# An expert-choice block and a routed block on one core: where the last pair's modulated products run, and when its shared experts run

## The chip, the core and the metric

The kernel runs on one core of one Trainium2 chip. The metric is device time in microseconds, the median of several executions; lower is better. The core has a matmul engine (PE; its weight loads are listed as PEld), a vector engine (DVE), an activation engine (ACT), a general engine (POOL) and a sync engine (SP), which issues most of the DMAs. Each engine works through its own queue in order, and engines wait for one another by semaphores.

## The reference

Eight sequences of 512 tokens with 256 features, fp32, pass through two residual layers.

```python
x = x + ffn0(adapter(x, language))      # 8 experts choose 128 tokens of each sequence
x = x + ffn1(conditioning(x))           # 64 experts, top 8 per token, 128 slots each
                                        # over all 4096 tokens, plus a shared expert
```

The conditioning is the part that matters here. For every sequence:

```python
ctx    = ema(x, tau_ctx)
gated  = x * sigmoid([x, ctx] @ Wg.T + bg)
mod    = 0.5 + sigmoid(gelu(x @ Wn1.T + bn1) @ Wn2.T + bn2)       # 512 x 8
traces = [ema(gated * mod[:, k:k+1], tau[k]) for k in range(8)]
temporal = sum(softmax(blend, 0)[k] * traces[k] for k in range(8))
soma   = gelu(x @ Wsoma.T + bsoma)
out    = layernorm((soma * sigmoid(temporal @ Wtemp.T + btemp)) @ Wout.T)
```

`ema` is the linear recurrence `h = alpha * h + b` along the tokens. Features lie on partitions, tokens along a row, so one recurrence over 128 features is one scan of 128x512. A sequence has 8 rates times 2 halves of the features, so 16 products `gated * mod * blend` and 16 scans. The shared expert of layer 1 is `(silu(x @ Wg) * (x @ Wu)) @ Wd` with 192 hidden features. The routed experts add their weighted results to the rows of their tokens.

## The kernel before

The sequences go in four groups of two. For every group PE first does eight experts of layer 0 (a "unit" is one expert of one group: L694 and L761, then two scatters by POOL, L779, which add the result to `x_rows` in DRAM). When a group's eight units have been scattered, `conditioning(b)` is run for its two sequences, interleaved with the next group's units: SP loads the rows (`xr`, L900), PE transposes them (L274), DVE scans the context `ct` (L959), PE and ACT make the gate (L977, L988), DVE makes `gx` (L996). The modulation `md` goes to DRAM and comes back spread over all partitions as `mdb` (L937 and L947, one load for each two rates). Then come the 16 modulated products `u` (L1037) and scans (L1048). For the first three pairs DVE adds the scans up (L1050); for the last pair, where no units follow, PE adds them in PSUM (L1065, `by_pe`). After this follow the gate of `temporal` (L1085, L1091, L1099), the output (L1120), the statistics and norm (L1133 to L1158), the router scores (L1181) and the shares of the top 8 (`taken`, L1199 to L1227).

`route(g)` collects each expert's tokens in 16 rounds on DVE (L1272, L1273) and a merge of two halves (L1291 to L1297); the second half's list comes by a DMA `rsecond` (L1304). The lists of all experts are turned by PE (L1348, `tkn`) to `ix_c` (L1351), which the first gather waits for.

`shared(b)` loads a sequence's transposed features (`rc1b`, L1372), runs three matmul groups (L1385), silu on ACT (L1391, L1393), a multiplication on DVE (L1397), two matmul groups (L1415), two copies to `rob` (L1420) and a store of the result into the DRAM tensor `odd` (L1429). `odd` and `out` are the two targets of the routed adds: expert e adds into `odd` if e is odd, else into `out`; the store of all eight shared results comes before the first add into `odd`.

`routed(e)` gathers 128 rows by POOL (L1486), transposes, multiplies, and adds by POOL (L1535). Weights come in pairs of experts, 1152 KB each: the first six pairs in a ring `wfar`, which a small POOL copy (L1448) holds back until the last `mdb` is in, and later ones in a ring `wnear` of `NEAR` buffers. `total(b)` reads `odd` and `out` at the end, adds them on DVE and writes `out`.

The order of the work on every engine is not written by hand. A list planner, `Order`, takes steps with an engine, a cost in microseconds, what they read and write, rings of buffers and a rank, and emits them as a simulated schedule starts them; `order.behind(s, x)` lets step `s` start only after `x` in that plan. On the chip only the resulting order of each queue and the semaphores remain. `LATE` names the sequences whose shared result is not stored into `odd` but kept in a buffer `xob` and added in `total`. It is empty here; the code for it is in the file, and for such a sequence zeros are stored to `odd` instead.

Of the kernel before, what the change touches and what calls it, by code (L numbers as in the profile page):

```python
# [8 lines left out]
F32 = mybir.dt.float32  # L9
I32 = mybir.dt.int32  # L10
U32 = mybir.dt.uint32
AF = mybir.ActivationFunctionType
ALU = mybir.AluOpType
# [4 lines left out]
P = 128  # L18
B, S, H = 8, 512, 256
T = B * S  # L20
NL, A = 10, 64
E0, K0, F0 = 8, 128, 1024
# [3 lines left out]
NH = H // P  # L26
PAIR = 2 * 2 * (H // P) * F1 + 3 * H
FAR = 6
NEAR = 8
SPREAD = 3  # L30
WARM = 6
LATE = ()
EPS = 1e-5
NEG = -3.0e38

# [117 lines left out]
def kernel(ctx: ExitStack, tc: tile.TileContext, d: dict, out: bass.AP):  # L153
    nc = tc.nc
# [4 lines left out]
    pools = {"ps": ctx.enter_context(tc.tile_pool(name="ps", bufs=2, space=PSUM))}  # L159
# [55 lines left out]

        "fw1": 2, "fw2": 2, "fb2": 2, "xg": 2 * 2, "exT": 2, "hf": 5, "y": 4,

        "xr": 1, "xb": 2, "hn": 1, "md": 1, "mdb": 5, "ct": 1, "th": 2, "gt": 2, "gx": 2, "so": 2, "tmp": 2, "u": 2, "tr": 2,
        "sg": 1, "c1": 1, "c1T": 1,

        "rlr": 2, "rtk": 1, "rm8": 2, "rev": 1, "rhalf": 1, "rsecond": 1, "rws": 1, "rc1b": 2, "rsl": 1, "rob": 1,

        "wfar": FAR, "wnear": NEAR, "xe": 8, "xhe": 4, "xeT": 3, "xsl": 2, "xheT": 2, "xye": 3, "xob": len(LATE),
    }
# [6 lines left out]
    order = Order(RINGS, ("mm", "hid", "res"))  # L231
    V = {}

    def tile_of(key, ring, shape, dtype=F32):
        place = WHERE.get(ring, "pc")
        if place not in pools:

            was, new = {"pc": (pa_cm, pc_cm), "pm": (pf_cm, pm_cm), "pw": (pc_cm, pw_cm)}[place]
            was.__exit__(None, None, None)
            pools[place] = new.__enter__()  # L240
        V[key] = pools[place].tile(shape, dtype, tag=ring, name=ring, bufs=RINGS[ring])
        return V[key]

    def bank(key, ring="mm"):
        return tile_of(key, ring, [P, 512])

    def pe(cost, fn, **k):
        return order.add("PE", cost, fn, **k)

    def act(cost, fn, **k):  # L250
        return order.add("ACT", cost, fn, **k)

    def dve(cost, fn, **k):
        return order.add("DVE", cost, fn, **k)

    def pool(cost, fn, **k):
        return order.add("POOL", cost, fn, **k)

    def load(size, fn, **k):
        return order.add("SP", 0.1, fn, size=size, **k)  # L260

    KB = 1024
# [38 lines left out]
    NG = len(GROUPS)  # L301
# [6 lines left out]
    def touch(t):  # L308

        nc.gpsimd.memset(t[(slice(0, 1),) * len(t.shape)], 0.0)  # L310
# [304 lines left out]


    units = [(g, e) for g in range(NG) for e in range(E0)]
    weights = []

    def expert(n):  # L620
        u = units[n]
        g, e = u
        bs = GROUPS[g]
        FILL, SOON = 1000 + n, 40
        w1, w2, b2, exT = (k + (u,) for k in (("fw1",), ("fw2",), ("fb2",), ("exT",)))

        def place_1():
            return tile_of(w1, "fw1", [P, NH, F0])

        def place_2():  # L630
            return tile_of(w2, "fw2", [P, NF, H])
# [12 lines left out]
        if n < 2:  # L644
            def hold():
                touch(place_1())
                touch(place_2())

            pool(0.2, hold, new=[(w1, "fw1"), (w2, "fw2")], rank=-1, after=first_rows[:4])
            load(512 * KB, load_1, w=[w1], rank=20 + n)  # L650
            load(512 * KB, load_2, w=[w2], rank=20 + n)
        else:
            weights.append(load(1024 * KB, load_1, new=[(w1, "fw1")], rank=20 + n))
            load(1024 * KB, load_2, new=[(w2, "fw2")], rank=20 + n)
        load(128 * KB, load_3, new=[(b2, "fb2")], rank=20 + n)

        which = 0 if bs[0] in groups[0] else 1
# [92 lines left out]
        for j, b in enumerate(bs):  # L750
            res, y = ("res", u, j), ("y", u, j)
            for part in range(2):
# [13 lines left out]
                need = [w2, b2, *dict.fromkeys(blocks[f][0] for f in fs)]  # L766
# [22 lines left out]
    W = {}  # L789
# [94 lines left out]
    def decay(k):  # L884
        return W["alpha"][:, k : k + 1].to_broadcast([P, S])
# [4 lines left out]
    def conditioning(b):  # L890
        rank = 100 + 5 * b
        g, j = where[b]
        pair = len(GROUPS[g]) == GB
        K = {k: (k, b) for k in (
            "xr", "xb", "hn", "md", "ct", "gx", "so", "tmp", "sg", "mv", "sd", "nm", "c1", "c1T",
        )}
# [8 lines left out]

        s = load(512 * KB, fetch, r=[("x1", b)], new=[(K["xr"], "xr")], rank=rank, after=last_adapter)

        for x in weights[E0 * (g + 1) :][:1]:
            order.behind(x, s)
        turned(K["xr"], K["xb"], "xb", rank, rank)  # L910


# [32 lines left out]
        for k in range(0, D1, 2):  # L945
# [6 lines left out]
            s = load(512 * KB, spread, r=[("md_rows", b)], new=[(("mdb", b, k), "mdb")], rank=rank)  # L952
# [15 lines left out]
        for ec in range(NH):  # L968
            pg, th = ("pg", b, ec), ("th", b, ec)
# [36 lines left out]
        for ec in range(NH):  # L1006
# [15 lines left out]
            new = [(ps, "mm")] + ([(K["so"], "so")] if ec == 0 else [])  # L1022
# [4 lines left out]
        by_pe = b in GROUPS[-1]  # L1027
        for k in range(D1):
            for hc in range(NH):
                mdb, tr, acc = ("mdb", b, k - k % 2), ("tr", b, k, hc), ("acc", b, hc)  # L1030
                tmp = (*K["tmp"], hc)

                def decayed(k=k, hc=hc, mdb=mdb, tr=tr, tmp=tmp):
                    if k == 0 and hc == 0:
                        V["tmp", b] = tile_of(K["tmp"], "tmp", [P, NH, S])
                    u = pools["pc"].tile([P, S], F32, tag="u", name="u", bufs=1)
                    nc.vector.scalar_tensor_tensor(  # L1037
                        u, V[K["gx"]][:, hc, :], W["blend"][:, hc, k : k + 1], V[mdb][:, k % 2, :],
                        ALU.mult, ALU.mult,
                    )  # L1040
                    whole = V[K["tmp"]][:, hc, :]
                    if by_pe:
                        t = tile_of(tr, "tr", [P, S])
                    elif k == 0:
                        t = whole
                    else:
                        t = pools["pc"].tile([P, S], F32, tag="t1", name="t1", bufs=1)
                    nc.vector.tensor_tensor_scan(t, decay(1 + k), u, 0.0, ALU.mult, ALU.add)  # L1048
                    if k and not by_pe:
                        nc.vector.tensor_tensor(whole, whole, t, ALU.add)  # L1050

                need = [K["gx"], mdb, "blend", "alpha"]
                cost = 2.05 if by_pe or k == 0 else 2.75
                if k == 0 and hc == 0:
                    dve(cost, decayed, r=need, new=[(K["tmp"], "tmp")] + ([(tr, "tr")] if by_pe else []),
                        w=[] if by_pe else [tmp], rank=rank)
                elif by_pe:
                    dve(cost, decayed, r=need, new=[(tr, "tr")], rank=rank)
                else:
                    dve(cost, decayed, r=[*need, K["tmp"]], w=[tmp], rank=rank)  # L1060
                if by_pe:
                    def gather_up(k=k, hc=hc, tr=tr, acc=acc):
                        if k == 0:
                            bank(acc, "res")
                        nc.tensor.matmul(V[acc], ident, V[tr], start=k == 0, stop=k == D1 - 1)  # L1065

                    if k == 0:
                        pe(1.0, gather_up, r=[tr], new=[(acc, "res")], rank=rank)
                    else:
                        pe(1.0, gather_up, r=[tr], w=[acc], rank=rank)  # L1070
# [7 lines left out]
        for ec in range(NH):  # L1078
            pgt, gt = ("pgt", b, ec), ("gt", b, ec)
# [15 lines left out]
            def mixed(ec=ec, gt=gt):  # L1095
# [8 lines left out]
               new=[(pgt, "mm"), (gt, "gt")], rank=rank)  # L1104
# [7 lines left out]
        for h, po in enumerate(halves):  # L1112
# [12 lines left out]
            new = [(po, "mm")] + ([(K["c1"], "c1")] if h == 0 else [])  # L1125
# [239 lines left out]
    def shared(b):  # L1365
        rank, soon, soon_dve = 2000 + b, 250 + b, 380 if b in LATE else 45
        c1T, ob = ("c1b", b), ("ob", b)
        ring = "xob" if b in LATE else "rob"

# [35 lines left out]
        for h in range(NC // 2):  # L1405
# [16 lines left out]
            new = [(po, "hid")] + ([(ob, ring)] if h == 0 else [])  # L1422
            lead = [pe(2.0, down, r=[("sh", 0), ("sh", 1), "wsd"], new=new, rank=rank, after=(lead if h else last_tokens if b in LATE else ()))]
            act(0.65, keep, r=[po], w=[ob], rank=soon)

        def store():

            src = zeros.unsqueeze(1).to_broadcast([P, NC, H]) if b in LATE else V[ob]
            nc.sync.dma_start(out=odd[b * S : (b + 1) * S, :].rearrange("(c p) h -> p c h", p=P), in_=src)  # L1429

        load(512 * KB, store, r=() if b in LATE else [ob], w=[("sum", 1, b)], rank=80 if b in LATE else rank)


    def pair(p):

        q = p - FAR
        ring = "wfar" if q < 0 or q % (FAR + NEAR) >= NEAR else "wnear"

# [16 lines left out]
        else:  # L1455
            load(PAIR * P * 3, fetch, new=[(("pair", p), ring)], rank=400 + 2 * p, after=last_tokens if p < FAR + NEAR else ())

# [9 lines left out]
    def give_up(e):  # L1467

        n, rest = divmod(e - 1, SPREAD)
        if e > 0 and rest == 0 and n + FAR + NEAR < E1 // 2:  # L1470
            def touched():
                nc.scalar.copy(spare, V["pair", n][:1, :1])
# [127 lines left out]
    for n in range(len(units)):  # L1600
        expert(n)
# [94 lines left out]
```

## Time and profile before

| | |
|---|---|
| median of 3 runs | 1174.95 us |
| lowest, highest | 1170.82, 1175.83 us |
| the profiled execution | 1181.5 us |
| its span | 1179.7 us |
| mean granted PE clock in it | 0.946 |
| PE busy | 1027.9 us, 87% |
| DVE busy | 682.0 us, 58% |
| ACT busy | 484.7 us, 41% |
| POOL busy | 382.1 us, 32% |
| DMA traffic | 221.75 MB, mean 188 GB/s |

The time is that of one execution as the device counts it. The span runs from the first to the last recorded instruction of the profiled execution; 1.8 us lie around it. Busy times count computing instructions, not waits and not the issue of plain DMAs; POOL's include its indirect DMAs, whose descriptors it prepares. In the lines of a timeline the columns are start, duration, engine, line and operation, output and inputs, the number of instructions, and in brackets the idle time of the engine before it with what ended it.

### The profile page before, as it was taken

Reading aid. Unit: us, or ns where it says so; the run is one execution under the profiler, and the core shown is the slowest. Engines: PE = TensorE matmul, PEld = TensorE weight load, DVE = VectorE, ACT = ScalarE, POOL = GpSimd, SP = SyncE. Lnnn points to the kernel's source line nnn. Section 1 sums busy time; section 2 is a strip of 40 time slices with the busy share of each in tenths; the row PEclk is TensorE's granted clock in tenths of the full one; section 3 lists DMA queues with packets and bytes.
Section 4 is the critical chain, followed back from the end, with each engine's and each line's share of the span. In section 5 each row is a group of like instructions: output and inputs, shape, how many; then the busy total and the mean of one; then the engine's idle time right before and its main releaser. Section 6 shows DMA issues by size and latency. Waiting matters only on the chain.

```text
span 1179.7 us, 13091 instructions
## 1 busy us (share of the span) xinstructions
PE 1027.9 (87%) x4325; PEld 758.5 (64%) x4325; DVE 682.0 (58%) x1447; ACT 484.7 (41%) x1029; POOL 382.1 (32%) x330
## 2 busy tenths in 40 slices
PE   7789999999989999989999999998985988887840
PEld 6578887857778776878676877434542655555530
DVE  3640236069882888974898947899574323332323
ACT  3474553343545534636444545423341423333200
POOL 7233123314222313322222312000002667776750
PEclk8789999899999999999999999999997999999875
DMA  9965556557456665546664633354176577777559
GB/s 285 346 196 170 166 166 179 153 190 270 131 166 179 201 233 177 169 113 218 198 225 124 204 99 93 128 218 183 58 266 236 142 212 183 210 202 230 123 97 379
DMA packets 89604, 221.75 MB, mean 188 GB/s; under 512 B 14896, under 2 KB 62488, under 8 KB 77120
## 3 DMA queue, kind: packets, MB, share of 16 engines
q1 hardware_dynamic: 63936, 183.91, 44.1%
q0 software_dynamic: 25600, 37.01, 16.4%
q8 instruction: 34, 0.56, 0.2%
q14 instruction: 34, 0.28, 0.1%
HBM read 177.69 MB, written 47.32 MB: 191 GB/s over the span
## 4 chain that ended last, share of the span: by engine, by line
PE 39%; DVE 30%; DMA 20%; issue 6%; ACT 2%; POOL 1%; SPq 0%; DVEq 0%; POOLq 0%; ACTq 0%
PE res L761 9%; PE hid L694 9%; DVE t L1048 8%; DVE u L1037 7%; DMA out_dram<-xye,ix_c 6%; DVE tmp L1050 4%; DVE tr L1048 3%; PE hid L1505 3%; PE mm L977 3%; DMA xe<-c_rows,ix_c 2%; DMA mdb<-md_rows 2%; PE mm L1085 2%; DMA odd<-xye,ix_c 2%; DMA rc1b<-c1T_rows 2%; PE hid L1385 2%
## 5 line engine op out<-in xcount | busy, mean ns | idle before, releaser
L694 PE MATMUL hid<-exT,fw 128*128 128x256 f32 x1024 | 234.4, 384 | 8.2 <-ACT hf L704 8.2
L761 PE MATMUL res<-fw,hf 128*128 128x256 f32 x1024 | 234.0, 380 | 0.0
L694 PEld LDWEIGHTS hid<-exT,fw 128*128 128x128 f32 x1024 | 195.1, 193 | 39.3 <-ACT hf L704 10.1
L761 PEld LDWEIGHTS res<-fw,hf 128*128 128x128 f32 x1024 | 192.1, 191 | 26.0 <-issue 1.4
L779 POOL DMA_INDIRECT x_rows<-y,ix x64 | 114.6, 1791 | 255.4 <-ACT y L776 249.2
L660 POOL DMA_INDIRECT xg<-c_rows,ix x64 | 68.3, 1067 | 221.1 <-PE hid L673 198.0
L704 ACT ACTIVATE hf<-hid,fb 128x256 f32<-128x256 f32 x256 | 104.8, 473 | 73.7 <-PE hid L694 73.5
L1532 DVE COPY xye<-res 128x256 f32<-128x256 f32 x64 | 27.2, 425 | 144.2 <-DMA out_dram<-xye,ix_c 69.2
L1048 DVE TENSOR_TENSOR_SCAN t<-alpha,u 128x512 f32<-128x512 f32 x84 | 102.8, 1224 | 2.9
L776 ACT ACTIVATE y<-y,gT 128x256 f32<-128x256 f32 x64 | 32.0, 508 | 169.6 <-DVE y L773 169.6
L1037 DVE SCALAR_TENSOR_TENSOR u<-gx,blend,mdb 128x512 f32<-128x512 f32 x128 | 95.4, 745 | 9.6 <-DMA mdb<-md_rows 8.7
L1486 POOL DMA_INDIRECT xe<-c_rows,ix_c x64 | 64.3, 1005 | 63.7 <-DVE ix_c L1351 42.7
L773 DVE TENSOR_TENSOR y<-res,fb 128x256 f32<-128x256 f32 x64 | 26.3, 418 | 75.0 <-PE res L761 74.9
L289 ACT ACTIVATE xeT<-mm,lgb 128x128 f32<-128x128 f32 x128 | 49.5, 456 | 41.6 <-PE mm L1495 34.4
L1508 ACT ACTIVATE xsl<-hid 128x192 f32<-128x192 f32 x64 | 21.2, 332 | 100.0 <-PE hid L1505 88.9
L1535 POOL DMA_INDIRECT out_dram<-xye,ix_c x32 | 50.4, 1575 | 29.2 <-DVE xye L1532 19.6
L1050 DVE TENSOR_TENSOR tmp<-tmp,t 128x512 f32<-128x512 f32 x84 | 58.2, 692 | 2.9
L289 ACT ACTIVATE exT<-hid,gains 128x128 f32<-128x128 f32 x128 | 48.1, 458 | 28.0 <-PE hid L673 25.8
L1535 POOL DMA_INDIRECT odd<-xye,ix_c x32 | 50.4, 1576 | 22.3 <-DVE xye L1532 11.7
L1385 PE MATMUL hid<-rc1b,wsgu 128*128 128x512 f32 x96 | 46.2, 619 | 12.9 <-DMA rc1b<-c1T_rows 12.9
L1505 PE MATMUL hid<-wnear,xeT 128*128 128x384 f32 x128 | 51.6, 530 | 0.0
L1505 PE MATMUL hid<-wfar,xeT 128*128 128x384 f32 x128 | 48.3, 507 | 0.8 <-ACT xeT L289 0.7
(227 smaller groups left out, 1577.7 us busy)
## 6 DMA issues: line engine op xcount, KB each, us to landing
fw<-in_fw_dram SPq DMA_DIRECT2D x64, 1024.0 KB
wfar<-in_wpair_dram SPq DMA_DIRECT2D x16, 1152.0 KB
wnear<-in_wpair_dram SPq DMA_DIRECT2D x16, 1152.0 KB
mdb<-md_rows SPq DMA_DIRECT2D x32, 512.0 KB
axb<-in_xT_dram SPq DMA_DIRECT2D x8, 512.0 KB
axt<-in_x_dram SPq DMA_DIRECT2D x8, 512.0 KB
fb<-in_fb_dram SPq DMA_DIRECT2D x32, 128.0 KB
x_rows<-axt SPq DMA_DIRECT2D x8, 512.0 KB
```

The costliest lines, as they stand in the source:

```text
L289: nc.scalar.activation(dst, src, AF.Identity, bias=gain[:, NH + hc : NH + hc + 1], scale=gain[:, hc : hc + 1])
L660: nc.gpsimd.indirect_dma_start(out=tile_of(("xg", u, b), "xg", [P, H]), out_offset=None, in_=c0_rows[b], in_offset=bass.IndirectOffsetOnAx ...
L694: nc.tensor.matmul(t[:, i, :], V[w1][:, hc, f * P : (f + 1) * P], V[exT][:, hc, :], start=hc == 0, stop=hc == NH - 1,)
L704: nc.scalar.activation(t[:, i, :], p[:, i, :], AF.Gelu_apprx_tanh, bias=fb1[:, e, f : f + 1])
L761: nc.tensor.matmul(V[res][:, :H], V[hf][:, i, j * K0 : (j + 1) * K0], V[w2][:, f, :], start=f == 0, stop=f == NF - 1,)
L779: nc.gpsimd.indirect_dma_start(out=x1_rows[b], out_offset=bass.IndirectOffsetOnAxis(ap=lists[b][0][:, e : e + 1], axis=0), in_=V[y], in_of ...
L1037: nc.vector.scalar_tensor_tensor(u, V[K["gx"]][:, hc, :], W["blend"][:, hc, k : k + 1], V[mdb][:, k % 2, :], ALU.mult, ALU.mult,)
L1048: nc.vector.tensor_tensor_scan(t, decay(1 + k), u, 0.0, ALU.mult, ALU.add)
L1050: nc.vector.tensor_tensor(whole, whole, t, ALU.add)
L1385: nc.tensor.matmul(t, W["wsgu"][:, hc, k * P : (k + 1) * P], V[c1T][:, hc, :], start=hc == 0, stop=hc == NH - 1)
L1505: nc.tensor.matmul(t[:, : 2 * F1], V[xeT][:, hc, :], wgu()[:, hc, :], start=hc == 0, stop=hc == NH - 1)
L1535: nc.gpsimd.indirect_dma_start(out=odd if j else out, out_offset=bass.IndirectOffsetOnAxis(ap=ix_c1[:, e : e + 1], axis=0), in_=V[ye], in_ ...
```

## The change

In the last pair (sequences 6 and 7), the product of `gx`, `blend` and `mdb` was one DVE instruction before each scan. Now, where `(k + hc) % 4` is not 0, so for 24 of the 32, POOL multiplies `gx` by `mdb` into a buffer of the new ring `up` (two buffers), ACT multiplies it in place by the column of `blend`, and DVE only scans. The ring `mdb` gives up a buffer (5 to 4).

`LATE` becomes (6, 7): the shared results of these two sequences stay in SBUF buffers `xob`, zeros are stored into `odd` in their place, near the beginning of the kernel, the second matmul groups of their shared experts come after the last token shares, and `total` adds the buffer with one more DVE addition. `NEAR` goes from 8 to 7. `total` of a late sequence reads and writes DRAM as `(c p) h`, rows of 1 KB, instead of `(p c) h`, rows of 4 KB.

In the planner's order both row loads of a pair went ahead of the first weights (`load_1`) of the third unit of the next group. Now the first sequence's rows go ahead of `load_1` of that group's second unit, and the second sequence's rows ahead of its `load_2`: one unit further ahead in SP's queue. In the last group no unit follows.

```diff
-NEAR = 8
+NEAR = 7
...
-LATE = ()
+LATE = (6, 7)
...
-        "xr": 1, "xb": 2, "hn": 1, "md": 1, "mdb": 5, "ct": 1, "th": 2, "gt": 2, "gx": 2, "so": 2, "tmp": 2, "u": 2, "tr": 2,
+        "xr": 1, "xb": 2, "hn": 1, "md": 1, "mdb": 4, "ct": 1, "th": 2, "gt": 2, "gx": 2, "so": 2, "tmp": 2, "u": 2, "up": 2, "tr": 2,
...
-    weights = []
+    weights = {}
...
-            weights.append(load(1024 * KB, load_1, new=[(w1, "fw1")], rank=20 + n))
-            load(1024 * KB, load_2, new=[(w2, "fw2")], rank=20 + n)
+            s1 = load(1024 * KB, load_1, new=[(w1, "fw1")], rank=20 + n)
+            weights[n] = s1, load(1024 * KB, load_2, new=[(w2, "fw2")], rank=20 + n)
...
-        for x in weights[E0 * (g + 1) :][:1]:
-            order.behind(x, s)
+        if g < NG - 1:
+            order.behind(weights[E0 * (g + 1) + 1][j], s)
...
+                uk = ("u", b, k, hc)
+                by_pool = by_pe and (k + hc) % 4 != 0
+                def product(uk=uk, k=k, hc=hc, mdb=mdb):
+                    nc.gpsimd.tensor_tensor(
+                        tile_of(uk, "up", [P, S]), V[K["gx"]][:, hc, :], V[mdb][:, k % 2, :], ALU.mult
+                    )
+                def blended(uk=uk, k=k, hc=hc):
+                    nc.scalar.activation(V[uk], V[uk], AF.Copy, scale=W["blend"][:, hc, k : k + 1])
...
+                    if by_pool:
+                        u = V[uk]
+                    else:
+                        u = pools["pc"].tile([P, S], F32, tag="u", name="u", bufs=1)
+                        nc.vector.scalar_tensor_tensor(
+                            u, V[K["gx"]][:, hc, :], W["blend"][:, hc, k : k + 1], V[mdb][:, k % 2, :],
+                            ALU.mult, ALU.mult,
+                        )
...
+                if by_pool:
+                    pool(1.65, product, r=[K["gx"], mdb], new=[(uk, "up")], rank=rank)
+                    act(0.7, blended, r=["blend"], w=[uk], rank=rank)
+                    need, cost = [uk, "alpha"], 1.25
```

## The prediction

> **What bounds the kernel now.** I read the table of windows first, because an average over the span mixes four different limits. Its columns are length, then busy time (and instructions) of PE, PEld, DVE, ACT and POOL, then granted clock, DMA share and GB/s.
>
> ```profile
> 755.00:792.00 37.00, 33.50 (x79) 13.10 (x77) 35.07 (x38) 10.00 (x14) 2.31 (x6) 1.00 0.47 169
> 792.00:838.00 46.00, 38.76 (x127) 21.37 (x127) 43.18 (x81) 17.56 (x25) 0.00 (x0) 1.00 0.47 183
> 838.00:905.00 67.00, 48.95 (x160) 28.12 (x159) 39.27 (x109) 20.27 (x31) 0.41 (x4) 0.90 0.54 207
> 905.00:950.00 45.00, 40.49 (x176) 28.29 (x174) 12.20 (x31) 19.45 (x54) 27.03 (x25) 1.00 0.60 168
> 950.00:1145.00 195.00, 153.18 (x628) 106.35 (x628) 59.73 (x164) 54.72 (x161) 138.13 (x104) 0.91 0.70 173
> 1145.00:1180.00 35.00, 0.00 (x0) 0.00 (x0) 9.77 (x8) 0.00 (x0) 0.00 (x0) 0.50 0.90 360
> ```
>
> From 90 to 735 us (not shown) PE is busy about 96%. In the last pair's modulated products, 755 to 838 us, DVE is busy 78.3 of 83 us, POOL 2.3. From 905 us POOL's queue of gathers and adds sets the pace. The last 35 us are a DMA tail. The timeline of DVE shows the first stage: a product, its scan, the next product, with gaps of about 0.1 us.
>
> ```profile
> 756.86 0.75 DVE L1037 SCALAR_TENSOR_TENSOR u<-gx,blend,mdb 128x512 f32<-128x512 f32 x1
> 757.64 1.22 DVE L1048 TENSOR_TENSOR_SCAN tr<-alpha,u 128x512 f32<-128x512 f32 x1
> 758.90 0.75 DVE L1037 SCALAR_TENSOR_TENSOR u<-gx,blend,mdb 128x512 f32<-128x512 f32 x1
> 759.76 1.23 DVE L1048 TENSOR_TENSOR_SCAN tr<-alpha,u 128x512 f32<-128x512 f32 x1
> ```
>
> One product and scan take 2.11 us (756.86 to 758.90, and on average). Sequence 6 ends at 791.95, sequence 7 at 838.25. PE's and POOL's timelines show the two places where the shared expert of a late sequence stands in the way: PE stands 12.91 us for a row load, and the first adds into `odd` wait for its store.
>
> ```profile
> 736.19 2.93 PE L1415 MATMUL hid<-wsd,sh 128*128 128x256 f32 x6 [2.67 <-DVE sh L1397]
> 738.91 1.21 PE L274 MATMUL mm<-ident,xr 128*128 128x128 f32 x8
> ```
> ```profile
> 898.63 5.88 PE L1385 MATMUL hid<-rc1b,wsgu 128*128 128x512 f32 x8 [12.91 <-DMA rc1b<-c1T_rows]
> 904.44 0.27 PE L1348 MATMUL mm<-ident,tkn 64*128 64x64 f32 x1
> ```
> ```profile
> 920.36 1.61 POOL L1535 DMA_INDIRECT out_dram<-xye,ix_c  x1 [2.68 <-DVE xheT L1523]
> 928.39 1.60 POOL L1535 DMA_INDIRECT out_dram<-xye,ix_c  x1 [2.98 <-DVE xye L1532]
> 936.51 1.63 POOL L1535 DMA_INDIRECT odd<-xye,ix_c  x1 [0.56 <-issue]
> 949.46 1.58 POOL L1535 DMA_INDIRECT odd<-xye,ix_c  x1 [3.63 <-DMA out_dram<-xye,ix_c]
> ```
>
> **The change part by part.** All in the profiled execution's own time: 1181.5 us, span 1179.7 plus 1.8 around it; the median of the runs is 1174.95, so I carry the difference over unchanged.
>
> *Start.* Two stores of zeros, 512 KB each, enter SP's queue near 6.6 us, ahead of the third sequence's `axb` and `axt`. From 0 to 10 us the DMA share is 0.62, from 10 to 50 us it is 1.05 at 363 GB/s. 1 MB at that rate is 2.9 us; whole if the later burst sets the start, nothing if the idle share takes it. I take +1.5 (0 to +3).
>
> *Middle pairs.* The rows' load goes ahead of both halves of a later unit's weights. A scatter that ended beside a weight load had its row load issued 7.3 us later (221.37 to 228.66); in the last pair, without one, 3.7 (728.60 to 732.34). PE takes the rows a quarter of a unit earlier, and its waits here are now small: 5.3 for `ct`, 3.3 for `tmp`, 0.7 for the rows over all three pairs. PE's work is unchanged. What SP is moved past: the weights of the next unit wait for the row loads, a unit ahead of their use (13.8 us of PE); if that cover goes, PE waits up to 3.7 a pair. I take +2 for the three pairs (-3 to +9).
>
> *Start of the last pair.* PE's order now has the transposes of sequence 6 directly after the first shared matmuls; L1415 with its 2.67 us wait is behind them. -2.4. The merge of the earlier route list on DVE (until 751.5) comes earlier too and frees nothing, since the wait for `md` ends later.
>
> *Products.* 24 of the 32 leave DVE: 24 x (0.75 + 0.10 gap) = -20.4. POOL multiplies, ACT scales in place, DVE scans. POOL has no arithmetic on two tensors in this trace. Nearest rows: a one-stream memset of 64x512 takes 0.52; memsets of 128x128 and 128x256 take 0.205 and 0.330, so 0.125 per 128 elements; a select with one read takes 0.293 on 128x128, 0.088 more. Two reads and one write of 512: 0.08 + 4 x (0.125 + 2 x 0.088) = 1.28. Ends: 0.52 and 1.58 (a scatter's duration). I take 1.28, being built from reads and writes.
>
> POOL is free then: 12 x 1.28 = 15.4 us in a sequence whose DVE chain is 12 x 1.33 + 4 x 2.11 = 24.4. But `up` has two buffers. One is held for product 1.28, ACT 0.65 (its 128x512 takes 0.59 to 0.69), scan 1.23 and three hand-overs, say 0.3: 3.5, so one scan per 1.73 us, and a sequence takes 24.4 to 12 x 1.73 + 8.4 = 29.2 instead of 33.8. For both: -9.2 to -18.8.
>
> A third limit is PE. In 755 to 838 us it works 72.3 us. The change moves two L1385 (1.73 each) and two L1415 groups (1.72) behind the last scan: 65.4 left. PE therefore forbids more than -18, and for that reason I count nothing for the second half's merge (3.0 us on DVE from 796.08), which leaves the chain as well. Between the ends I take -14. ACT's 24 scalings are 15.6 us; it was busy 27.6 of the 83, and its queue is in order, so a scaling can wait behind a gate's activation; that is in the 14.
>
> The Trainium skill, page "GPSIMD Engine Reference", section 3.1, gives 4497 ns for a sum of 2048 fp32 elements; a quarter, as an estimate, is 1.12 us, and with it the ring's pitch would be 1.67 instead of 1.73.
>
> The same skill, "SBUF — State Buffer", section "Who interferes with whom", speaks against this change: a VectorE instruction with two SBUF inputs and a GpSimd instruction that reads SBUF exclude one another, the second to start waits. The scan has two inputs from SBUF. By the rule every POOL product stops DVE, and the sum's -14 becomes 24 x 1.12 - 20.4 = +6.5, an estimate. No row here shows the two side by side.
>
> *To the first gather (838 to 905 us).* The chain stats, norm, `taken`, 16 rounds, merge, second half's load stays. Fewer multiplications lie between the rounds (4 at 0.69), `wnear` has seven loads instead of eight, but the transpose of `tkn` now stands behind shared(6), whose row load is behind `wnear`: seven loads of 1152 KB at the 340 GB/s of 870 to 898 us land 24 us after issue, `tkn` is ready 31 after. -1 (-4 to +4).
>
> *Routed stage.* The adds into `odd` need no store of shared(7) any more. From first gather to the sixth add went 44.2 us (905.25 to 949.46). The first add came 15.1 after the first gather; five more at the later pitch of 3.31 (58 steps from 949.46 to 1141.37) make 31.7: -12.5. Against it the matmuls of shared(7) and part of shared(6), 8.6 us a sequence (5.2 + 3.5), enter PE there. PE needs 2.86 per expert, POOL 3.21, so the slack takes some. +6.5. Sum -6 (-12 to +3).
>
> *Tail.* Two more DVE adds of 128x1024 (1.23 each, as 9.8/8) before the last sequences' sums, and rows of 1 KB instead of 4: +1 (0 to +3).
>
> Sum: 1.5 + 2 - 2.4 - 14 - 1 - 6 + 1 = -18.9, so 1174.95 - 18.9 = **1156.0**.
>
> **The rivals.**
>
> *POOL and DVE exclude each other* (slower). Place: the 24 products. Price t each, 24t - 20.4. The other terms sum to -4.9, so no gain is left from t = 1.05, and over 0.5% (5.9 us, about what a measurement of this kernel tells from no change) is lost from t = 1.30. At 1.28: +10.3 - 4.9 = 1180.4; at 1.58: 1187.6. For it: DVE and POOL have never both streamed SBUF here. Against it: scans beside POOL's descriptor work keep 1.22 us, a weak witness.
>
> *The ring or ACT paces the products* (smaller gain). A buffer cycle of 4.2 gives 2.1 per scan, the old pitch; then only the DVE-free gaps gain, say -5: total -9.9, 1165.
>
> *The routed stage gives nothing back.* PE worked 193.7 of the 240 us from 905 to 1145; 12 more still fit, but the first ten experts come when PE is 90% busy. The term becomes 0: 1162. *PE waits in the middle* at +9 and with start +3: 1164.5.
>
> **How the numbers follow.** Forecast 0.55; ring or ACT 0.15; routed or middle terms lost 0.12; exclusion 0.18, a third of it within 0.5%. The small gains (1162 to 1165) are over 0.5% but near; I put 0.05 of them within. Faster 0.77, same 0.11, slower 0.12. Low end: products -18, routed -12, start 0, middle -1: 1174.95 - 34 = 1141. High end: the exclusion at its price, 1180; beyond it 0.1 at most, below 1141 about 0.1.
>
> **What would show it.** `up` on POOL near 1.28 us beside scans that keep 1.23; DVE's last scan near 820 us instead of 838; PE near 95% busy in that stretch; sixth routed add some 38 us after the first gather, not 44. Wrong would be: POOL products or scans stretched beyond 2 us, gaps before scans over 0.8 us ended by ACT, a first gather less than 8 us earlier, or PE waiting on `fw` or `ct` by more than 3 us a pair before 735.

## The result

The changed kernel takes as long as the one before: 1174.18 us against 1174.88 (medians of 20 runs each, 1167.36 to 1182.04 and 1166.44 to 1181.94), a ratio of 0.9999 with a 95% interval of 0.9975 to 1.0023. Twelve more runs of it on another chip gave 1.0012 (0.9987 to 1.0036). The forecast of 1156, with a gain of over 0.5% at 0.77, was wrong.

The first profiled execution of the changed kernel lasted 1172.96 us (span 1171.2). This is the table of windows of its trace, same columns and same stretches as for before:

```profile
755.00:792.00 37.00, 32.75 (x81) 13.42 (x79) 31.30 (x22) 15.94 (x24) 21.65 (x12) 1.00 0.38 128
792.00:838.00 46.00, 41.04 (x123) 20.63 (x123) 41.14 (x58) 25.46 (x37) 22.97 (x19) 1.00 0.61 226
838.00:905.00 67.00, 53.57 (x175) 32.66 (x174) 39.91 (x110) 21.45 (x33) 3.12 (x7) 0.90 0.55 207
905.00:950.00 45.00, 42.12 (x171) 28.34 (x170) 13.81 (x36) 16.76 (x47) 32.27 (x28) 0.96 0.66 174
950.00:1145.00 195.00, 151.04 (x639) 105.22 (x637) 60.79 (x159) 56.35 (x170) 129.81 (x99) 0.94 0.73 188
```

In the first two stretches, those of the products, DVE has 80 instead of 119 records, but only 5.8 us less busy time (72.4 instead of 78.3). POOL went from 2.3 to 44.6. The timelines of DVE and then POOL, at the start of the products, show why:

```profile
759.76 2.17 DVE L1062 TENSOR_TENSOR_SCAN tr<-alpha,u 128x512 f32<-128x512 f32 x1
761.86 2.22 DVE L959 TENSOR_TENSOR_SCAN ct<-alpha,xb 128x512 f32<-128x512 f32 x1
...
780.90 1.23 DVE L1062 TENSOR_TENSOR_SCAN tr<-alpha,u 128x512 f32<-128x512 f32 x1
...
802.16 1.80 DVE L1062 TENSOR_TENSOR_SCAN tr<-alpha,up 128x512 f32<-128x512 f32 x1
```
```profile
759.04 3.96 POOL L1037 TENSOR_TENSOR up<-gx,mdb 128x512 f32<-128x512 f32 x2 [23.54 <-DMA mdb<-md_rows]
...
783.32 1.63 POOL L1037 TENSOR_TENSOR up<-gx,mdb 128x512 f32<-128x512 f32 x1 [4.39 <-DVE tr L1062]
...
801.61 1.27 POOL L1037 TENSOR_TENSOR up<-gx,mdb 128x512 f32<-128x512 f32 x1 [4.39 <-DVE tr L1062]
```

A scan beside POOL's products lasts 2.17 or 2.22 us; at 780.90, while POOL is idle, 1.23. A product lasts 1.27 us at 801.61, where DVE runs a multiplication with one operand in PSUM, and 1.98 on average at 759.04, beside a DVE product and two scans. The one that starts second is the one that waits: the scan at 802.16 begins 0.55 us after that product of 1.27 and lasts 1.80; the product at 770.67 begins 0.16 us after a scan of 1.19 and lasts 2.10.

The other places shown in the prediction: PE now waits 4.14 us for the rows and 8.00 for `rc1b`, and the adds into `odd` no longer wait (first PE's timeline, then POOL's):

```profile
741.26 1.38 PE L274 MATMUL mm<-ident,xr 128*128 128x128 f32 x8 [4.14 <-DMA xr<-x_rows]
742.44 3.30 PE L1433 MATMUL hid<-wsd,sh 128*128 128x256 f32 x8
...
892.12 5.33 PE L1403 MATMUL hid<-rc1b,wsgu 128*128 128x512 f32 x8 [8.00 <-DMA rc1b<-c1T_rows]
```
```profile
916.18 1.61 POOL L1553 DMA_INDIRECT out_dram<-xye,ix_c  x1 [0.60 <-DVE xheT L1541]
...
919.39 1.60 POOL L1553 DMA_INDIRECT odd<-xye,ix_c  x1 [0.30 <-issue]
...
934.82 1.60 POOL L1553 DMA_INDIRECT odd<-xye,ix_c  x1 [0.30 <-issue]
```

The first add into `odd` follows the first gather (901.68) by 17.7 us; before it was 31.3, and the sixth add of all, at 934.82, follows it by 33.1.

One execution differs from another by up to 15 us, so the stretches below are means over three traces of the changed kernel and two of before. The stretches end at the last scatter of layer 0, the first product on DVE, the end of the last scan, the first gather, the sixth add, the last add, and the end.

| stretch | before (two traces) | changed (three traces) | difference |
|---|---|---|---|
| to the last scatter | 730.5, 727.4 | 733.9, 728.8, 731.2 | +2.3 |
| to the first product | 24.3, 22.8 | 25.0, 25.5, 25.1 | +1.7 |
| the products | 83.4, 83.4 | 77.5, 77.5, 77.5 | -5.9 |
| to the first gather | 67.0, 67.2 | 65.2, 65.3, 65.1 | -1.9 |
| to the sixth add | 44.2, 40.0 | 33.1, 33.9, 34.2 | -8.4 |
| sixth to last add | 191.9, 190.1 | 196.8, 197.5, 197.5 | +6.3 |
| to the end | 38.4, 38.9 | 39.6, 39.1, 39.2 | +0.7 |

They sum to -5.2; the medians say -0.7. The three traces of the changed kernel are executions of 1169 to 1173 us, below its medians of 1174 and 1177, and one of the two of before took 1181.5, well above its median of 1174.88, so some 4 us of this table are the choice of executions. The stretches that agree to some tenths between executions (the products, to the first gather) can be relied on; the first one can't, by itself.

### The profile page after: what moved, and what is told of

The parts are those of the page before. It is cut to its first block, busy times and chain, and to the rows that moved or that the text cites. A ratio compares the mean times of both kernels' runs of the same rounds, so it can differ in the third digit from the quotient of the medians.

```text
span 1171.2 us, 13104 instructions
## 1 busy us (share of the span) xinstructions
PE 1032.2 (88%) x4325; PEld 762.2 (65%) x4325; DVE 682.7 (58%) x1425; ACT 493.2 (42%) x1049; POOL 422.4 (36%) x354
## 4 chain that ended last, share of the span: by engine, by line
PE 43%; DVE 22%; DMA 19%; issue 10%; POOL 2%; ACT 2%; SPq 1%; DVEq 0%; POOLq 0%; ACTq 0%
PE res L761 9%; PE hid L694 9%; DVE t L1062 6%; DMA odd<-xye,ix_c 6%; DVE u L1051 4%; PE hid L1523 4%; DVE tmp L1064 3%; DMA x_rows<-y,ix 3%; DVE tr L1062 2%; PE mm L1103 2%; PE hid L1403 2%; PE mm L1138 2%; PE mm L977 2%; DMA rc1b<-c1T_rows 2%; PE res L1546 2%
## 5 line engine op out<-in xcount | busy, mean ns | idle before, releaser
L694 PE MATMUL hid<-exT,fw 128*128 128x256 f32 x1024 | 234.9, 385 | 10.6 <-ACT hf L704 10.6
L779 POOL DMA_INDIRECT x_rows<-y,ix x64 | 112.2, 1754 | 304.9 <-ACT y L776 298.2
L1051 DVE SCALAR_TENSOR_TENSOR u<-gx,blend,mdb 128x512 f32<-128x512 f32 x104 | 78.2, 752 | 2.7 <-DMA mdb<-md_rows 2.4
L1553 POOL DMA_INDIRECT odd<-xye,ix_c x32 | 51.0, 1593 | 27.1 <-DMA odd<-xye,ix_c 13.6
L1037 POOL TENSOR_TENSOR up<-gx,mdb 128x512 f32<-128x512 f32 x24 | 40.1, 1685 | 51.8 <-DVE tr L1062 28.1
L1523 PE MATMUL hid<-wfar,xeT 128*128 128x384 f32 x144 | 54.6, 505 | 0.0
```

The lines of the kernel that those rows point to most:

```text
L694: nc.tensor.matmul(t[:, i, :], V[w1][:, hc, f * P : (f + 1) * P], V[exT][:, hc, :], start=hc == 0, stop=hc == NH - 1,)
L779: nc.gpsimd.indirect_dma_start(out=x1_rows[b], out_offset=bass.IndirectOffsetOnAxis(ap=lists[b][0][:, e : e + 1], axis=0), in_=V[y], in_of ...
L1051: nc.vector.scalar_tensor_tensor(u, V[K["gx"]][:, hc, :], W["blend"][:, hc, k : k + 1], V[mdb][:, k % 2, :], ALU.mult, ALU.mult,)
L1523: nc.tensor.matmul(t[:, : 2 * F1], V[xeT][:, hc, :], wgu()[:, hc, :], start=hc == 0, stop=hc == NH - 1)
L1553: nc.gpsimd.indirect_dma_start(out=odd if j else out, out_offset=bass.IndirectOffsetOnAxis(ap=ix_c1[:, e : e + 1], axis=0), in_=V[ye], in_ ...
```

## The experiments

The change has three parts that can be taken alone: P, the products by POOL and ACT; R, the rows' loads one unit further ahead; L, the late shared experts with seven near buffers. All ratios are against runs of before on the same chip, with 95% intervals; the stretches are in us, from one trace each except in the last two rows. All these kernels keep the smaller ring of four `mdb` buffers; L alone, which has it too, shows no loss from it.

| kernel | ratio | products | first gather to sixth add | sixth to last add |
|---|---|---|---|---|
| P | 1.0132 (1.0109 to 1.0156) | 85.0 | 53.2 | 191.2 |
| R | 1.0057 (1.0037 to 1.0078) | 81.7 | 53.8 | 190.9 |
| L | 1.0005 (0.9983 to 1.0027) | 83.5 | 32.4 | 198.3 |
| R, L | 1.0015 (0.9986 to 1.0043) | 82.2 | 36.8 | 203.1 |
| P, R | 1.0082 (1.0059 to 1.0105) | 77.5 | 53.0 | 192.2 |
| P, L | 1.0102 (1.0071 to 1.0133), again 1.0035 (1.0009 to 1.0060) | 85.1 | 34.2 | 199.2, 193.8 |
| P, R, L | 0.9999 (0.9975 to 1.0023), again 1.0012 (0.9987 to 1.0036) | 77.5 | 33.7 | 197.3 |

**P alone.** Against the changed kernel:

```diff
-NEAR = 7
+NEAR = 8
-LATE = (6, 7)
+LATE = ()
...
-            order.behind(weights[E0 * (g + 1) + 1][j], s)
+            order.behind(weights[E0 * (g + 1) + 2][0], s)
```

> Products by POOL and ACT alone (nothing late, eight near buffers, rows' loads as before, four mdb buffers). Theory 1, POOL's products and DVE's scans shut one another out: scans beside a product take 2.1 to 2.3 us instead of 1.23, the 32 products take 75 to 83 us from first product to last scan instead of 83.4, and the kernel is -6 to +3 us against before. Theory 2, the products are worth their forecast and another part of the change gives it back: the products' stretch is 69 us or less and the kernel 10 to 15 us faster than before.

It is 1.3% slower than before. The shut-out is there (the scans of `up` take 1.35 us on average, POOL's products 1.73), and the stretch, 85.0, is even longer than without POOL: DVE waits 10.5 us in it for ACT's scaled products, 3.9 in the changed kernel. The merge of the previous route list (second half, at 765.9) lies inside it, but it does in before too (2.6 us of DVE), so the merge alone does not make it longer than 83.4. The larger loss is elsewhere and neither theory had it: from the first gather to the sixth add 53.2 us. In the planner's new order the last matmuls of sequence 7's shared expert come between those of the routed experts; they end at 947.9, and only then can its result be stored into `odd`: the store is issued at 948.57, 39.8 us after the first gather, in before's two traces 26.5 and 24.3 after it. Until then no odd expert can be added. POOL's timeline of this kernel:

```profile
929.68 1.62 POOL L1553 DMA_INDIRECT out_dram<-xye,ix_c  x1 [0.73 <-DVE xye L1550]
...
952.72 1.61 POOL L1553 DMA_INDIRECT odd<-xye,ix_c  x1 [7.94 <-issue]
```

**R and L, all products on DVE** (`by_pool = False`, everything else as changed).

> The change with all 32 products left on DVE. Theory 1: within 4 us of the changed kernel, since the products brought about 6 us at most. Theory 2: 10 to 15 us slower than the changed kernel, so slower than before by about as much. In both the routed stage's first six adds take about 30 us from the first gather, as in the changed kernel, not 44.

By the ratios within 2 us of before and of the changed kernel, as the first theory had it. Between this kernel and the changed one, whose other work in this stretch has nearly the same order, it goes from 82.2 to 77.5: 4.7 us is what 24 products on POOL are worth here. Their forecast was 14. The sixth add comes 36.8 us after the first gather here and 33.7 in the changed kernel, not about 30 in both.

The next stretch takes even this back. From the last scan to the first gather this kernel needs 58.8 us and the changed one 65.2, so from the last scatter of layer 0 to the first gather they need 165.9 and 167.9. Most of the 6.4 us is one place on PE. In the changed kernel DVE has finished `tkn` at 895.86, but PE turns it only at 900.84, since its queue has a late sequence's matmuls first, which began at 892.12 after 8.00 us of waiting for their rows. Here the rows ahead of `tkn` were loaded before the `wnear` weights (issued at 868.00 and 870.60, in the changed kernel at 871.54 and 868.07), PE is through with their matmuls at 889.3, and it turns `tkn` 0.06 us after it is there. First DVE and PE of the changed kernel, then of this one:

```profile
895.58 0.28 DVE L1363 SCALAR_TENSOR_TENSOR tkn<-tkn,list 64x128 f32<-64x128 f32 x1
...
897.29 3.62 PE L1433 MATMUL hid<-wsd,sh 128*128 128x256 f32 x16
900.84 0.27 PE L1366 MATMUL mm<-ident,tkn 64*128 64x64 f32 x1
```
```profile
897.53 0.28 DVE L1363 SCALAR_TENSOR_TENSOR tkn<-tkn,list 64x128 f32<-64x128 f32 x1
...
897.87 0.37 PE L1366 MATMUL mm<-ident,tkn 64*128 64x64 f32 x1 [8.60 <-DVE tkn L1363]
```

The wait of `tkn` for PE is 4.8 to 5.0 us in all three traces of the changed kernel and 3.5 in both of before; a kernel with the changed products and this matmul order was not run.

**P and R, nothing late** (`LATE = ()`, `NEAR = 8`).

> The change without the late shared experts (nothing late, eight near buffers); products and rows as changed. Theory 1: the late part is worth what the two traces show in the routed stage, -6 us net, so this kernel is 3 to 8 us slower than the changed one. Rival, the late part gives back what it takes: the first six adds are 14 us faster but the later adds run at a longer pitch, and this kernel is within 2 us of the changed one.

0.8% slower than before, 53.0 us to the sixth add: the store of sequence 7's shared result is issued at 945.39. So L is needed as soon as P or R is there, and undoes what they cause in the routed stage.

**P and L, rows as before** (the last pair of lines of the first diff).

> The change with the rows' loads where they were in the queue. If the new place costs PE the 4 us by which the last unit ended later in the changed kernel's trace: 2 to 4 us faster than the changed kernel, and the last unit of layer 0 ends near 728 us instead of 732. If that delay is the zeros at the start, or the scatter of one execution against another: within 2 us of the changed kernel.

Slower instead of faster. This was not understood from six runs and one trace (its shortest execution), so it was taken again.

> The change with the rows' loads where they were, once more (only 6 runs of it were taken, and its trace was its shortest). If its 10 us over the changed kernel are the kernel's, the median is 1182 to 1185 again and a longer trace shows where: in the products' stretch (85.1) or in the routed stage. If they were an accident of few runs, it comes out near the late experts alone, 1177 to 1179.

With 12 runs the loss is 0.35%, less than the first figure, and its interval still lies above 1. Both traces show the same place: 85.1 us of products. With the rows one unit ahead the route list is merged at 737.3 and 744.8, ahead of the products; here (first trace) at 746.7 and 763.2, the second inside them. As with P alone this is a part only, for L alone has the merge inside too and takes 83.5: in both traces DVE waits 10.5 us for ACT's scaled products, beside 3.9 with the rows moved. So with the old rows the 24 products on POOL cost 1.6 us instead of bringing 4.7. Why they wait longer there was not tried.

**R alone** (`by_pool = False`, `LATE = ()`, `NEAR = 8`).

> The rows' loads one unit further ahead alone (all products on DVE, nothing late, eight near buffers). In the traces so far every kernel with this part takes 4.4 us more from the first pair's units to the last scatter (170.5, 170.8 and 169.4 us for the three later groups instead of 169.6, 168.8 and 168.0). Theory: it costs that here too, with nothing to earn it back but about 1 us in the products' stretch: 3 to 8 us slower than before. Rival: it gains in the last pair by the merges that leave its stretch: within 2 us of before or faster.

0.57% slower. From the first pair's last scatter (the 8th unit) to the last scatter it takes 510.6 us, and in the eleven traces with R 509.2 to 511.3, in the seven without 504.7 to 508.1. The means are 510.6 and 506.9: R costs 3.7 us in the middle pairs. In this stretch PE stands idle 17.8 us on average with R (16.7 to 19.0) and 15.5 without (13.9 to 16.9). It is not one wait more but others: from 223 to 731 us PE waits 5.3 us for `ct` in before and not at all in the changed kernel, but 10.6 instead of 7.3 for `hf` (ACT) and 5.3 instead of 3.3 for `tmp`. The other 1.4 us are PE's busy time, 492.8 instead of 491.4, and go with the granted clock of the execution: 490.0 us at 0.997, 494.3 at 0.987, and 493.0 at 0.990 in a trace without R. Whether R has a part in that clock was not tried. The rest of its loss is again the store of sequence 7 (53.8 us to the sixth add, 11.7 more than before), and, in its one trace, a start of the last pair that is 4.2 longer; the stretch to the first gather gives 5.6 back.

**L alone** (`by_pool = False`, rows as before).

> The late shared experts alone (all products on DVE, rows as before, seven near buffers). Theory: from the first gather to the sixth add 30 to 34 us instead of 35 to 44, given back by about 4 to 8 us more between the sixth and the last add: -4 to +3 us against before. If the late experts were worth 6 us by themselves, as forecast: 4 us or more faster.

No difference that can be measured: 9.7 us less to the sixth add than the mean of before's two traces, 7.3 us more from there to the last.

**Repeats of before and of the changed kernel.**

> The kernel before, once more, for a second trace of it: how far its stretches differ from one execution to another. The two traces at hand differ by 8.5 us between the kernels, the medians by 0.7; if the first trace of before was a long one, this one is shorter by about 6 us, and the place where it is shorter is the place of the scatter.

> The changed kernel, once more, for a second trace: product stretch 77 to 78 us and first gather to sixth add 30 us again if these belong to the kernel and not to one execution; the units before them and the adds after the sixth may differ by some us.

> The changed kernel, once more, on the same chip as the two above: within 3 us of before; stretch 77.5 us, sixth add 33 to 34 us after the first gather.

The second execution of before was 1171.61 us long, 9.9 shorter than the first: 3.1 to the last scatter, 1.5 in the pair's start, 4.2 to the sixth add and 1.8 after it. The 44.2 us that the forecast of the routed stage started from was a long one; the other trace has 40.0. The repeats of the changed kernel took 1169.41 us and, on the chip of the last comparison, 1171.6 in the profiled execution.

**What shuts out what.** The product is kept, but ACT writes its scaled result to PSUM:

```diff
-                    nc.scalar.activation(V[uk], V[uk], AF.Copy, scale=W["blend"][:, hc, k : k + 1])
+                    nc.scalar.activation(bank((uk, "ps")), V[uk], AF.Copy, scale=W["blend"][:, hc, k : k + 1])
...
-                        u = V[uk]
+                        u = V[uk, "ps"]
...
-                    act(0.7, blended, r=["blend"], w=[uk], rank=rank)
-                    need, cost = [uk, "alpha"], 1.25
+                    act(0.7, blended, r=[uk, "blend"], new=[((uk, "ps"), "mm")], rank=rank)
+                    need, cost = [(uk, "ps"), "alpha"], 1.25
```

> The changed kernel, but ACT writes its scaled product into a PSUM bank (ring of the other small matmul results) instead of back into the SBUF buffer, so the scan has one input from SBUF and one from PSUM. If POOL's reads and a second SBUF input of DVE shut one another out, scans beside POOL's products go back to about 1.25 us, the products to 1.27, and the stretch from first product to last scan falls from 77.5 to about 68 us; the kernel 6 to 10 us faster than the changed one. If DVE and POOL slow each other in some other way (writes, any SBUF use), scans stay at 2.1 to 2.3 beside products and the time stays within 3 us of the changed kernel.

Groups of this kernel between 750 and 842 us (busy, mean ns of one, then idle time before them):

```profile
L1037 POOL TENSOR_TENSOR up<-gx,mdb 128x512 f32<-128x512 f32 x24 | 35.7, 1512 | 48.1 <-DMA mdb<-md_rows 23.5 <-ACT mm L1042 12.6 <-DVE gx L996 12.0
...
L1062 DVE TENSOR_TENSOR_SCAN tr<-alpha,mm 128x512 f32<-128x512 f32 x24 | 28.2, 1206 | 4.4 <-ACT mm L1042 2.2 <-PE res L1083 2.0
...
L1062 DVE TENSOR_TENSOR_SCAN tr<-alpha,u 128x512 f32<-128x512 f32 x8 | 12.5, 1563 | 0.8
...
L959 DVE TENSOR_TENSOR_SCAN ct<-alpha,xb 128x512 f32<-128x512 f32 x2 | 4.5, 2268 | 0.0
```

and the scans of the changed kernel in the same view:

```profile
L1037 POOL TENSOR_TENSOR up<-gx,mdb 128x512 f32<-128x512 f32 x24 | 40.1, 1685 | 51.8 <-DVE tr L1062 28.1 <-DMA mdb<-md_rows 23.5 <-ACT gt L1109 0.2
L1062 DVE TENSOR_TENSOR_SCAN tr<-alpha,up 128x512 f32<-128x512 f32 x24 | 33.1, 1410 | 4.2 <-ACT up L1042 3.9 <-PE res L1083 0.2
```

The 24 scans that read PSUM take 1.21 us beside POOL, as if it were not there. In the same kernel the scans with both inputs in SBUF (`u`, `ct`) still go up to 1.56 and 2.27 on average, and they still stretch the products to 1.51. So the condition is a second input of DVE from SBUF, not its work as such. The stretch falls from 77.5 to 72.3, not to 68, and the kernel is faster than before: 0.9963 (0.9938 to 0.9988). Once more, on another chip:

> The changed kernel with the scaled products in PSUM, once more, beside the changed kernel on the same chip: 3 to 6 us faster than it, products' stretch 72.3 us.

0.9969 (0.9944 to 0.9994), 72.3 us again, beside 1.0012 for the changed kernel there.

**POOL writing without reading** (the products left out).

```diff
-                    nc.gpsimd.tensor_tensor(
-                        tile_of(uk, "up", [P, S]), V[K["gx"]][:, hc, :], V[mdb][:, k % 2, :], ALU.mult
-                    )
+                    nc.gpsimd.memset(tile_of(uk, "up", [P, S]), 0.01)
```

> The changed kernel with the 24 products left out: POOL writes a constant of the same size into the buffer instead (so the output differs), which writes SBUF as the product does and reads nothing. If it is POOL's reading that shuts DVE out, scans keep 1.23 us and the write takes about 0.6 us; if any POOL use of SBUF does, scans beside it grow by that 0.6.

The scans keep their 1.21 to 1.23 us, the writes take 0.52. One run took 1159.3 us, beside a median of 1171.76 for before. The stretch is 65.1 us. Groups, and then the window of just that stretch:

```profile
L1060 DVE TENSOR_TENSOR_SCAN tr<-alpha,up 128x512 f32<-128x512 f32 x24 | 28.3, 1211 | 4.9 <-PE res L1081 2.9 <-ACT up L1040 2.0
L1037 POOL MEMSET up<- 128x512 f32 x22 | 11.5, 524 | 69.1 <-DVE tr L1060 63.4 <-DMA out_dram<-x_rows 5.1 <-DVE rs L1162 0.6
```
```profile
757.20:822.40 65.20, 64.33 (x191) 33.08 (x190) 56.16 (x77) 38.59 (x59) 12.55 (x28) 1.00 0.59 218
```

PE is busy 64.33 of 65.20 us, and DVE's scans now wait for PE's bank (`res`). So PE is the next bound of the pair when nothing shuts DVE out.

**More buffers for the products** (`"up": 3`).

> The changed kernel with three buffers for POOL's products instead of two. The prediction held that two buffers pace the scans at 1.73 us. If the number of buffers is what holds the stretch at 77.5 us, it falls by 4 us or more and the waits for the scaled product go; if the shut-out of scans and products is, it stays at 76 to 79 us and the time within 3 us of the changed kernel.

77.8 us, and 1.0019 (0.9989 to 1.0048): nothing. The waits of the scans for ACT's result are gone, and the scans and products are longer instead: these groups are from 750 to 842 us of this kernel.

```profile
L1037 POOL TENSOR_TENSOR up<-gx,mdb 128x512 f32<-128x512 f32 x24 | 44.2, 1861 | 49.6 <-DMA mdb<-md_rows 23.5 <-DVE tr L1062 22.7 <-ACT so L1020 1.8
L1062 DVE TENSOR_TENSOR_SCAN tr<-alpha,up 128x512 f32<-128x512 f32 x24 | 34.4, 1459 | 1.2 <-PE res L1083 0.6 <-ACT rsl L1411 0.5
```

**PSUM with the old place of the rows, and PSUM with all 32 products** (`by_pool = by_pe`).

> The scaled products in PSUM, with the rows' loads where they were before. If what the new place of the rows costs (4.4 us) is a loss that only the shut-out of DVE's merges by POOL's products earned back, this kernel is 3 to 6 us faster than the one with the products in PSUM and the rows moved, so 8 us or more faster than before. If the merges in the products' stretch cost as much on their own, within 3 us of it.

0.9985 (0.9963 to 1.0008), not faster than with R: the stretch is 80.4, 8.1 more than with R. The merge, in it again, takes 4.6 of them on DVE; the rest are mainly longer waits, for ACT's gate above all (4.4 us instead of 0.6). About what R costs in the middle, it earns here.

> The changed kernel with all 32 products by POOL and their scaled results in PSUM. DVE has then only scans with one SBUF input. If DVE is what is left to shorten, the stretch from first scan to last goes from 72 to about 66 us, where PE's work lies (the kernel without the products' reads stood at 65.1), 4 to 6 us faster than with 24. If POOL's own pace comes in (32 of 1.27 us and the hand-overs to ACT), the stretch stays at 71 to 74 us and the time within 2 us of it.

0.9994 (0.9971 to 1.0016). The 32 scans take 1.21 us and the products only 1.33, so DVE and POOL hardly meet any more, but the first scan comes 29.5 us after the last scatter, having to wait for a product and for ACT, and the stretch from there is 72.4: the scans wait 6.2 us for ACT's results and 3.7 for PE's bank, and `sg` 5.5 for ACT's gate.

## Why the prediction was wrong

**Products (-14, measured -5.9, of which 4.7 for the products alone).** This is the step that failed; it makes 8.1 of the 13.7 us between the forecast -18.9 and the -5.2 of the stretches. The price of a product by itself was right (1.28 forecast, 1.27 alone), and so was PE's limit (65.4 forecast, 65.1 with the products' reads left out). Wrong was the choice of the forecast for the meeting of the two engines: it let scan and product run side by side. The exclusion that was put as a rival is what happens, though not at its price. 24t - 20.4 = -4.7 gives t = 0.65: about half of each product's 1.27 us held DVE up, the rest lay beside DVE work with an operand in PSUM, beside small instructions and beside DVE's waits. The busy times say the same: against the kernel with all products on DVE, DVE's falls only from 76.0 to 71.3 us in the stretch, though 24 products of 0.75 and two L1415 have left it, so its other instructions became some 14 us longer. At the first gather nothing is left of the 4.7 us: the kernel without POOL's products is there 2.0 us sooner after the last scatter. The ring of two buffers, which made the lower bound of that step, was not a limit here: three changed nothing. With the old rows, where the scans wait 10.5 us for their operand, three were not tried.

The rule of the Trainium skill ("SBUF — State Buffer", "Who interferes with whom") was weighed in the prediction and put second, because no row of before showed it. The runs agree with its three parts: two inputs from SBUF against a reading POOL exclude one another (1.23 to 2.17 us), one input does not (1.21), a POOL instruction that only writes does not (1.21). The prediction drew from the rule that every product stops DVE, hence +6.5; in the trace the second to start waits, often the product itself, and the products brought 4.7 us. The page "GPSIMD Engine Reference", section 3.1, led to an estimate of 1.12 us; the trace has 1.27.

**Start of the last pair (-2.4, measured +1.7).** Half the step was right: the transposes no longer stand behind the L1415 with its wait. But they wait 4.14 us for the rows, and the eight matmuls that were put behind them (L1433, 3.30 us) lie ahead of L917, so L917 starts 4.3 us after the transposes instead of 2.8. The prediction moved the matmuls off one path and did not look at the next instruction behind their new place.

**Routed stage (-6, measured -2.1).** To the sixth add -8.4 against a forecast -12.5: 2.1 of the difference are the base, since 44.2 was one long execution and the mean of two is 42.1, and 2.0 are that the sixth add came 33.7 us after the first gather instead of 31.7. After it +6.3, as forecast (+6.5), though not shown to be by PE: in the changed kernel POOL's waits between 930 and 1145 us are led by the landing of earlier adds into `odd` (13.6 us), in before by DVE's copies (28.3 in its first trace). What makes the adds' pitch 197.3 / 58 = 3.40 us instead of 3.29 stays open. From the first gather to the last add before takes 236.1 and 230.1 us and the changed kernel 229.9 to 231.8, so a gain of this stage as a whole is shown only against the longer execution.

**Middle and start (+3.5, measured +2.3 in three traces against two).** R costs 3.7 over all traces, near the forecast +2 and within its range, but not by the forecast's way: it counted waits for `ct`, `tmp` and the rows and let PE wait for weights, while what grew were the waits for `tmp` and for `hf`, which it did not list (7.3 us in before's trace). The two scatters that its working calls ended, at 221.37 and 728.60, start at these times. The zeros cost nothing that can be seen: the 8th unit's scatter comes at 219.8 to 225.1 us in the five traces without them, 219.6 to 227.0 in the thirteen with them. **Tail** +0.7 for +1 was right.

**To the first gather (-1, measured -1.9).** The number was near by luck. The prediction held the late sequence's row load harmless, since it would land 24 us after the weights' issue and `tkn` be ready 31 after. PE did go on after 24.1 us (868.07 to 892.12), and `tkn` was ready after 27.8, but 8.7 us of that sequence's matmuls (892.12 to 900.84) stand between the rows and the transpose of `tkn`, and no term had them. `tkn` waits 4.8 to 5.0 us for them. (The 340 GB/s used there is what the eight loads make of the 28 us from 870 to 898; all traffic was 395.)

**What was not in the prediction at all** is that the parts need one another. Alone, P and R each lose, because in the order that the planner then makes sequence 7's shared expert comes so late that the odd adds wait for its store; L removes that store, and alone is worth nothing. R alone loses in the middle, and with P and L earns it back in the products' stretch, 77.5 us instead of 85.1: the merge leaves it (3.6 us), and DVE's waits for ACT's scaled products fall from 10.5 to 3.9.

## What to carry to other kernels

Before work is moved from DVE to POOL, look where DVE's operands lie: with both in SBUF and POOL reading SBUF, the moved work is hidden only in part, here by about half, and DVE pays for the rest; one operand in PSUM frees it, here at the price of a changed destination of an ACT instruction. Work out where an instruction that leaves a path lands, and who is next behind it: here L917 in one place and the transpose of `tkn`, which the first gather waits for, in another. And take the base of a forecast from two executions where a stretch depends on what lands when: 44.2 and 40.0 us were the same kernel.

## What the runs showed of the hardware

A scan of 128x512 with both inputs in SBUF took 1.23 us alone and 2.10 to 2.22 beside a POOL product of two SBUF tensors; the product went from 1.27 to 1.69 on average, 2.18 at most. With the second input in PSUM the scan took 1.21 us beside the same products, and beside POOL writes of the same size (0.52 us) that read nothing it took 1.21 from SBUF.
